# Context values of the last key block: three 32-column pieces beside self-attention in place of part of each values step in cross-attention

## The chip, the cores and the metric

The kernel runs on one core of a Trainium2 chip. The metric is the device time of one execution in microseconds (us). Beside the timed runs there is one profiled execution; its span runs from the first to the last instruction, and its own time is a little longer than the span.

The engines are named as in the profile: PE multiplies matrices (PEld are its weight loads), DVE, ACT and POOL work on vectors, and SP issues transfers (DMA). Each engine works through its own list in the order in which the program wrote it.

## The reference, cut to what matters

One transformer block on `x` (2 batches, 1024 rows, 256 columns, fp32) with a context (2 batches, 154 rows, 192 columns). 16 heads of 64 columns. Cut to its core:

```python
h = _layernorm(x, ln1_g, ln1_b)
x = _attention(h, h, sa_wq, sa_wk, sa_wv, sa_wo, sa_bo) + x
h = _layernorm(x, ln2_g, ln2_b)
x = _attention(h, cond_emb, ca_wq, ca_wk, ca_wv, ca_wo, ca_bo) + x
h = _layernorm(x, ln3_g, ln3_b)
a, gate = jnp.split(h @ ff_w1 + ff_b1, 2, axis=-1)
x = (a * gelu(gate)) @ ff_w2 + ff_b2 + x
```

In the second attention keys and values come from the context: `v = cond_emb @ ca_wv`, 154 rows of 1024 columns for each batch. The change concerns how these values are made.

## The kernel before, in words

**Stages.** Self-attention runs from about 17 to 710 us, cross-attention to about 918 us, the gated feed-forward to the end. All work is fp32, and every list is written out by hand, so that the order of the Python calls is the order on each engine.

**Self-attention.** The outer loop goes over 128 slots `p`. Eight slots make a unit, and a unit is one batch and one pair of heads (16 units, `ui`, counted from 0; units 0 to 7 are batch 0). I count the slots of a unit from 0 as `n`. Each slot computes scores of two row groups (L483, 32 matmuls in 64x32 tiles, into two PSUM tiles named `s`), then DVE takes their maximum (L645), ACT the exponents (L494), and one slot later the two halves of the keys are joined: a transfer exchanges maxima and sums (L504, SP), POOL computes `dd`, `zz` and `den` (L512 to L520), ACT `ee` (L516), DVE a reciprocal (L591), and POOL scales (L595). DVE turns the probabilities (L609) two slots after their scores.

What stands between two slots' scores on PE depends on `n`. In slots 2, 3, 6 and 7 it is the product with the values (`weigh`, L530). In slots 0, 1, 4 and 5 `run_work` puts in work of the next unit: queries, keys (both L352) and values (L383) in slots 0, 1 and 4, and in slot 5, from unit 2 on, two output pieces (`out_piece`, L457), whose results DVE adds to `x` some slots later (L464). Steps of the next normalization go beside them in slots 4 and 5. POOL adds biases (L310) in some slots. `load_ahead` issues the next weights on SP (L132) in slots 2, 3 and 7. All small accumulators live in two pools of two PSUM banks each, `mm_tile` and `sum_tile`; L530 uses both banks of `sum_tile`.

**Cross-attention.** 48 slots `c`, three per unit. A slot computes scores (L772), DVE the maximum (L777), ACT the exponents (L788), POOL scales (L799), and DVE turns (L815) into a ring `pT_ca` of three units. SP regroups a unit's turned probabilities with eight transfers (L832). The product with the values (`cross_values`, L851, results `poc`) of unit `ui` stands in the second slot of unit `ui + 2`, in 64x64 tiles, in two parts: the first takes the two banks of `sum_tile`, the second those of `mm_tile`. DVE copies the results out (L864).

The 154 keys are held as five blocks of 32 (the last one padded). Blocks 0 to 3 are weighed in regrouped pairs; the last block is weighed from the ring directly, and its values must stand on all four groups of 32 partitions.

**`context_values`** (L723 to L756) makes the values of two pairs of heads (256 columns) of one batch. It is called eight times: for unit 0 near the end of self-attention, and for units 2, 4, ... 14 in the second slot of the unit. It clears two planes of the tile `v` on DVE (L729) and runs four matmuls of 96x128 weights and 256 moving columns (L733): two for keys 0 to 127, and two for keys 32 to 159, of which only the last block is used. ACT copies the first 128 keys out (L742, two halves) and the last block from partitions 96 to 127 (L743). Then SP issues two transfers for the other halves (L745) and three that spread the last block over the other partition groups (L750). These go through the list `later`, from which each slot takes two entries.

In the second slot of an even unit, PE's order around it is: one output piece (L457, into `sum_tile`), `context_values` (L733, into `mm_tile`), a second output piece (L457, `mm_tile`), then `cross_values` (L851). DVE adds the two output pieces (L464) after clearing `v`.

**Weights.** `load_weights("ca", pr, "v")` loads 256 columns of `ca_wv` for each call. `load_keys` loads columns of `ca_wk` into a buffer with the tag `ck` for `context_keys` (L717), in self-attention's unit 0 and again in unit 14.

The lines that the change alters:

```python
        for n, k0 in enumerate((0, TP - P)):
            for c in range(2):
                nc.tensor.matmul(
                    pv[:, n * VC:(n + 1) * VC], lhsT=ctxT[:, c, b * TP + k0:b * TP + k0 + P],
                    rhs=wsl["ca", pr, "v"][:, c, :], start=(c == 0), stop=(c == 1),
                )
```

Of the kernel before, what the change touches and what calls it, by code (L numbers as in the profile page):

```python
# [8 lines left out]
F32 = mybir.dt.float32  # L9
# [4 lines left out]
P = 128  # L14
# [4 lines left out]
def tile_transformer_block(ctx: ExitStack, tc: tile.TileContext, a: dict, out: bass.AP):  # L19
    nc = tc.nc  # L20
    x, cond = a["x"], a["ctx_768"]
    w = {k[len("L0_xattn_"):]: v for k, v in a.items() if k.startswith("L0_xattn_")}

    B, S, D = x.shape
    T, DC = cond.shape[1:]
    DA = w["sa_wq"].shape[1]
    DF = w["ff_w2"].shape[0]
    DH = 64
    NPAIR = DA // (2 * DH)
# [6 lines left out]
    HR = P // 2  # L36
    NH = D // HR
    CC = DC // 2
    KP = T // 2
    KB = 32  # L40
    NB = -(-T // KB)
    VC = 2 * P
    HB = 512
    QG = 2 * KB
    TP = NB * KB
    NM = P // QG
# [5 lines left out]
    SH = GH // 2  # L52
# [4 lines left out]
    const = ctx.enter_context(tc.tile_pool(name="const", bufs=1))  # L57
    one = ctx.enter_context(tc.tile_pool(name="one", bufs=1))
    wpool = ctx.enter_context(tc.tile_pool(name="w", bufs=1))
# [8 lines left out]
    def mm_tile(name):  # L68
        return ps_m.tile([P, HB], F32, tag="mm", name=name)
# [36 lines left out]
    for n in names[:2]:  # L106
        for r0 in range(0, P, HR):
            (nc.scalar if n == names[0] else nc.sync).dma_start(
                out=cols[r0:r0 + HR, row_of[n]:row_of[n] + NH],
                in_=w[n].rearrange("(r p) -> p r", p=HR),  # L110
# [13 lines left out]
    def load_slice(name, c0, n, p):  # L124

        own = w[name][:, c0:c0 + n]
        if p != HR:
            return load_rows(wpool, name[3:], f"{name}_{c0}", own, p)
        t = wpool.tile(
            [P, NH, n], F32, tag=name[3:], name=f"{name}_{c0}", bufs=2 if name[3:] == "wq" else 1)  # L130
        for r0 in range(0, P, HR):
            nc.sync.dma_start(out=t[r0:r0 + HR], in_=own.rearrange("(c p) f -> p c f", p=HR))  # L132
        return t

    wsl, wo = {}, {}

    def load_weights(kind, pr, what):
        if kind == "sa" or what == "q":
            wsl[kind, pr, what] = load_slice(f"{kind}_w{what}", pr * P, P, HR)
        elif pr % 2 == 0:  # L140
            wsl[kind, pr, what] = load_slice(f"{kind}_w{what}", pr * P, VC, CC)

# [22 lines left out]
    for n in names[2:]:  # L165
        own = rows[row_of[n] - n_cols:row_of[n] - n_cols + n_of[n], :]
        p = HR if n in twice else P
# [13 lines left out]
    ctxT = const.tile([CC, 2, B * TP], F32, tag="ctxT", name="ctxT")  # L181
# [10 lines left out]
    def turn_context(b):  # L192
        pc = spare["bank"](f"pc{b}")
        for c in range(2):
            for i in range(2):
                nc.tensor.transpose(
                    pc[:CC, c * T + i * KP:c * T + (i + 1) * KP],
                    cn[b][:, i, c * CC:(c + 1) * CC], ident[:KP, :KP],
                )
        return lambda: nc.scalar.copy(  # L200
            ctxT[:, :, b * TP:b * TP + T], pc[:CC, :2 * T].rearrange("p (c k) -> p c k", c=2)
        )

    hT, vs, qk, oT = {}, {}, {}, {}

# [338 lines left out]
    def run(piece):  # L544
        done = piece()
        if done is not None:
            (adds if getattr(done, "adds", False) else stores).append(done)
# [165 lines left out]
    def context_keys(pr, bank):  # L713
# [6 lines left out]
            )  # L720
        return lambda: nc.scalar.copy(kT[:, pr, :], pk[:, :B * TP])

    def context_values(b, pr):  # L723

        v = vs["ca", b, pr // 2] = pt_.tile([P, NM + 2, VC], F32, tag="V", name=f"v_ca{b}_{pr}")
        nc.vector.memset(v[:, NM:, :], 0.0)  # L729
        pv = mm_tile(f"pv_ca{b}_{pr}")  # L730
        for n, k0 in enumerate((0, TP - P)):
            for c in range(2):
                nc.tensor.matmul(  # L733
                    pv[:, n * VC:(n + 1) * VC], lhsT=ctxT[:, c, b * TP + k0:b * TP + k0 + P],
                    rhs=wsl["ca", pr, "v"][:, c, :], start=(c == 0), stop=(c == 1),
                )
        last = P // KB - 1

        def store():
            for n in range(NM):  # L740
                own = slice(n * QG, (n + 1) * QG)
                nc.scalar.copy(v[own, n, :], pv[own, :VC])  # L742
            nc.scalar.copy(v[last * KB:, NM + last % 2, :], pv[last * KB:, VC:])  # L743
            later.insert(0, lambda: [
                nc.sync.dma_start(  # L745
                    out=v[(1 - n) * QG:(2 - n) * QG, n, :], in_=v[n * QG:(n + 1) * QG, n, :])
                for n in range(NM)
            ])
            later.insert(1, lambda: [
                nc.sync.dma_start(  # L750
                    out=v[a4 * KB:(a4 + 1) * KB, NM + a4 % 2, :],
                    in_=v[last * KB:, NM + last % 2, :])
                for a4 in range(last)
            ])

        return store  # L756
# [5 lines left out]
    def cross_first(c):  # L762
# [19 lines left out]
        def then():  # L782
            pr_ = pp_.tile([P, 2, TG, NB * KB], F32, tag="P", name=f"p_{c}")
            nc.gpsimd.memset(pr_[:, :, :, T:], 0.0)
# [50 lines left out]
    def cross_values(ui, a2):  # L835
# [10 lines left out]
        for m in range(NM + 1):  # L846
            for a4 in quarters:
                r0 = a4 // 2 * QG
                r = slice(r0, r0 + QG)
                for j in range(2):  # L850
# [3 lines left out]
                        rhs=pTc["pairs"][r, a2, m, j] if m < NM else  # L854
                        pTc["ring"][r, ui % 3, NB - 1, j, :],
                        start=(m == 0), stop=(m == NM),
# [121 lines left out]
    with tc.manual_schedule():  # L978
# [11 lines left out]
        own = [ps_s.tile([P, 2, HB], F32, tag="s", name=f"first_{r}") for r in range(2)]  # L990
# [45 lines left out]
        for p in range(SA):  # L1036
            if p % (2 * SH) == 0:
                self_beside(p // (2 * SH))
            if p == SA - SH:
                work.extend(held)  # L1040
                held.clear()
            then = self_first(p)
            flush(stores)
            late = then()
            if p >= LAG:
                turn_groups(p - LAG)
            if adds:
                adds.pop(0)()
            if late:
                late()  # L1050
            flush(kept)
            if later and (p < 4 or p % (2 * SH) in (2, 4, 6)):
                later.pop(0)()
            if p in ahead:
                ahead[p]()
            load_ahead(p)
            h, hg = divmod(p, SH)
            if h == 0 or hg < LAG:

                run_work(2 if p < SA - SH else 1, h % 2 or h == 0, sum_tile)  # L1060
                if p == LAG:
                    load_weights("sa", units[1][1], "v")
                ui, n = divmod(p, 2 * SH)
                if n == SH + 1 and ui in (1, NU - 1):

                    pr = 0 if ui == 1 else 3
                    run(lambda: context_keys(pr, sum_tile))
                    kept.extend(context_keys(pr + i, mm_tile) for i in range(1, 3 if ui == 1 else 2))
            else:
                run(lambda: self_values(h - 1, hg - LAG))  # L1070

        for c in range(CA):
            if c == 0:
                pTc["ring"] = pt_.tile(
                    [P, 2 * NK, QH // 2], F32, tag="pT", name="pT_ca"
                ).rearrange("p a b -> p (a b)")[:, :3 * 2 * NB * NT * KB].rearrange(
                    "p (u n j q) -> p u n j q", u=3, n=NB, j=2)
            if c == SH + 1:
# [7 lines left out]
            ui, n = divmod(c, len(CG))  # L1086
# [52 lines left out]
            elif n == 2:  # L1139
# [3 lines left out]
                elif ui == HP:  # L1143
                    wo["ca"] = const.tile([P, NPAIR, D], F32, tag="wo", name="ca_wo")
                    later[:0] = [lambda i=i: nc.sync.dma_start(
                        out=wo["ca"][:, i, :], in_=w["ca_wo"][i * P:(i + 1) * P, :])
# [6 lines left out]
        for k in range(FF):  # L1153
            c = CA + k
# [57 lines left out]
```

## Time and profile before

| what | us |
|---|---|
| three timed runs, median (lowest, highest) | 1115.72 (1113.64, 1117.36) |
| the profiled execution's own time | 1111.62 |
| its span | 1109.7 |
| PE busy, share of the span | 1093.7, 99% |
| DVE busy | 855.1, 77% |
| ACT busy | 628.2, 57% |
| POOL busy | 681.4, 61% |
| PE busy in 17 to 710 / 722 to 918 / 918 to 1110 | 685.5 / 195.5 / 188.3 |
| DVE busy in the same | 633.0 / 151.3 / 53.1 |

The granted TensorE clock is 1.00 throughout. PE's 99% is not PE at its peak: matmuls overlap, and their ends are modelled. A group in the profile reads: line, engine, operation, what it writes and reads, shapes and count, then busy us, mean ns of one, and the idle time of the engine before them with what ended it. Before the shapes stands the tile of the array that a PE instruction uses (64*32 is 64 rows by 32 columns). A timeline line reads: start in us, length in us, engine, line, operation, count, and in brackets the idle time before it and what ended that. "issue" is a pause for which the profile shows no wait.

### The profile page before, as it was taken

The numbers are of one execution on the slowest core, as the hardware profiler recorded it, in microseconds if no ns is written. First come the engines' busy times: TensorE is split into PE (matmuls) and PEld (weight loads), VectorE is DVE, ScalarE is ACT, GpSimd is POOL, SyncE is SP. The second block draws the span as 40 slices with busy tenths as digits, with TensorE's granted clock in tenths as the row PEclk, the third lists the DMA queues.
The fourth block names the chain that finished last, engine by engine and source line by source line (L and its number), as shares of the span: only waits on it lengthen the run. The fifth ranks groups of instructions, "written<-read, shape, count | busy, mean of one in ns | idle before, by whom it ended". The sixth has DMA issues, their size and how long they took to land.

```text
span 1109.7 us, 44860 instructions
## 1 busy us (share of the span) xinstructions
PE 1093.7 (99%) x18436; PEld 733.5 (66%) x18436; DVE 855.1 (77%) x1205; ACT 628.2 (57%) x2030; POOL 681.4 (61%) x1584
## 2 busy tenths in 40 slices
PE   8999999999999999999999999999999999999998
PEld 6555656546556566666566565576766777888887
DVE  5889999898999899999999999868777875322222
ACT  4766666766666666667667666655556553121111
POOL 2777877777877787777777777756656653220000
PEclk9999999999999999999999999999999999999999
DMA  3222212111111012011111111136665443000000
GB/s 83 67 59 57 56 28 52 43 41 42 25 40 42 23 42 47 13 43 42 23 42 33 32 33 28 38 87 158 167 164 126 113 107 77 10 11 10 20 10 19
DMA packets 102350, 59.66 MB, mean 54 GB/s; under 512 B 31994, under 2 KB 92930, under 8 KB 102146
## 3 DMA queue, kind: packets, MB, share of 16 engines
q1 hardware_dynamic: 100914, 56.15, 21.3%
q8 instruction: 145, 2.38, 0.9%
q10 hardware_dynamic: 1232, 0.66, 0.2%
q14 instruction: 59, 0.48, 0.1%
HBM read 27.12 MB, written 2.10 MB: 26 GB/s over the span
## 4 chain that ended last, share of the span: by engine, by line
PE 56%; ACT 11%; DVE 10%; POOL 8%; DMA 7%; issue 4%; SPq 4%; DVEq 0%; POOLq 0%; ACTq 0%
PE pa L933 10%; ACT p L494 10%; PE po L530 8%; PE s L483 8%; DVE st L645 6%; DMA st<-st 6%; PE py_ca L457 5%; PE pf L956 5%; PE pq_ca L352 4%; PE poc L851 4%; SPq L504 3%; POOL p L595 3%; PE sc L772 3%; PE py_sa L457 2%; PE pk_sa L352 2%
## 5 line engine op out<-in xcount | busy, mean ns | idle before, releaser
L494 ACT ACTIVATE p<-s,st 128x512 f32<-128x512 f32 x512 | 344.9, 686 | 194.0 <-DVE st L645 186.0
L595 POOL TENSOR_SCALAR p<-p,rd,ee 128x512 f32<-128x512 f32 x512 | 385.7, 768 | 46.7 <-DVE rd L591 45.4
L645 DVE TENSOR_REDUCE st<-s 128x2 f32<-128x1024 f32 x256 | 300.9, 1216 | 20.3 <-PE s L483 7.1
L609 DVE STREAM_TRANSPOSE pT<-p 128x1024 f32<-128x1024 f32 x256 | 302.3, 1218 | 0.3 <-POOL p L595 0.3
L483 PE MATMUL s<-k_sa,q_sa 64*32 64x512 f32 x4096 | 262.1, 592 | 7.4 <-ACT p L494 6.5
L530 PE MATMUL po<-pT,v_sa 64*32 64x256 f32 x8192 | 239.5, 376 | 0.9 <-DVE pT L609 0.9
L530 PEld LDWEIGHTS po<-pT,v_sa 64*32 64x32 f32 x8192 | 177.9, 106 | 70.5 <-issue 22.0
L483 PEld LDWEIGHTS s<-k_sa,q_sa 64*32 64x32 f32 x4096 | 78.8, 106 | 115.2 <-ACT p L494 66.4
L799 POOL TENSOR_SCALAR p<-p,rden 128x154 f32<-128x154 f32 x256 | 96.8, 398 | 76.0 <-DVE rden L796 75.6
L788 ACT ACTIVATE p<-sc,neg 128x154 f32<-128x154 f32 x256 | 96.2, 405 | 83.1 <-DVE rden L796 78.0
L942 DVE SCALAR_TENSOR_TENSOR u<-pa,cols,gate 128x256 f32<-128x256 f32 x64 | 31.0, 484 | 123.1 <-ACT gate L939 123.1
L933 PE MATMUL pa<-hT_ln,wf 128*128 128x256 f32 x512 | 121.1, 380 | 0.2 <-ACT p L788 0.2
L939 ACT ACTIVATE gate<-pa,cols 128x256 f32<-128x256 f32 x64 | 30.3, 474 | 147.8 <-PE pa L933 146.1
L933 PEld LDWEIGHTS pa<-hT_ln,wf 128*128 128x128 f32 x512 | 96.7, 190 | 14.0 <-issue 0.8
L494 ACT ACTIVATION_READ_ACCUMULATOR p<-s,st 128x1 f32 x512 | 103.8, 203 | 0.0
L383 PEld LDWEIGHTS pv_sa<-sa_wv,hT_ln 64*128 64x128 f32 x1024 | 59.0, 188 | 14.6 <-issue 5.9
L956 PE MATMUL pf<-wf,u 128*128 128x256 f32 x256 | 64.7, 379 | 0.0
L518 POOL TENSOR_TENSOR zz<-ee,st 128x8 f32<-128x8 f32 x128 | 25.9, 202 | 61.5 <-ACT ee L516 61.5
L383 PE MATMUL pv_sa<-sa_wv,hT_ln 64*128 64x128 f32 x1024 | 62.4, 276 | 0.1
L457 PE MATMUL py_sa<-sa_wo,o_sa 128*128 128x256 f32 x256 | 59.7, 385 | 0.0
L457 PE MATMUL py_ca<-ca_wo,o_ca 128*128 128x256 f32 x256 | 59.7, 381 | 0.0
L457 PEld LDWEIGHTS py_sa<-sa_wo,o_sa 128*128 128x128 f32 x256 | 47.3, 190 | 17.9 <-ACT v_sa L392 8.4
(87 smaller groups left out, 1265.4 us busy)
## 6 DMA issues: line engine op xcount, KB each, us to landing
wf<-pT_ca SPq DMA_DIRECT2D x128, 128.0 KB, 2.4
st<-st SPq DMA_DIRECT2D x512, 1.0 KB, 1.8
v_sa<-v_sa SPq DMA_DIRECT2D x32, 256.0 KB, 3.5
sa_wq<-in_L_xattn_sa_wq_dram SPq DMA_DIRECT2D x32, 128.0 KB, 3.0
sa_wk<-in_L_xattn_sa_wk_dram SPq DMA_DIRECT2D x32, 128.0 KB, 3.0
sa_wv<-in_L_xattn_sa_wv_dram SPq DMA_DIRECT2D x32, 128.0 KB, 3.1
ca_wq<-in_L_xattn_ca_wq_dram SPq DMA_DIRECT2D x32, 128.0 KB, 3.3
wf<-in_L_xattn_ff_w_dram SPq DMA_DIRECT2D x12, 256.0 KB, 4.0
```

The lines of the kernel that those rows point to most:

```text
L383: nc.tensor.matmul(pv[r][:, i * P:(i + 1) * P], lhsT=h[own, c, i * P:(i + 1) * P], rhs=wt[own, c, :], start=(c == 0), stop=(c == NH - 1), ...
L457: nc.tensor.matmul(py[:, e * D:(e + 1) * D], lhsT=o[:, i, (t + e) * P:(t + e + 1) * P], rhs=wo[kind][:, g * HP + i, :], start=(i == 0), st ...
L483: nc.tensor.matmul(sc[a4 * KB:(a4 + 1) * KB, j, :], lhsT=q[r, c:c + KB], rhs=k[r, h * HB:(h + 1) * HB], start=True, stop=True, tile_positi ...
L494: nc.scalar.activation(pr[:, j, :], sc[:, j, :], AF.Exp, bias=st[:, 0, 0, i, j:j + 1], accum_out=st[:, 0, 1, i, j:j + 1],)
L530: nc.tensor.matmul(po[a2][d:d + KB, :QH // 2], lhsT=v[r, t, e, d:d + KB], rhs=pT[r, d // DH * NK + n, :], start=(t == 0 and e == 0), stop= ...
L595: nc.gpsimd.tensor_scalar(pr[:, j, :], pr[:, j, :], rd[:, c:c + 1], ee[:, 0, c:c + 1], op0=ALU.mult, op1=ALU.mult,)
L609: nc.vector.transpose(halves[h][:, :, c:c + KB], groups.pop(0).rearrange("p j (n k) -> p (j n) k", k=KB))
L645: nc.vector.tensor_reduce(st[:, 0, 0, i, :], sc[i], AX.X, ALU.max, negate=True)
L788: nc.scalar.activation(pr_[:, j, i, :T], sc[:, j, i * T:(i + 1) * T], AF.Exp, bias=neg[:, j, i:i + 1], accum_out=den[:, j, i:i + 1],)
L799: nc.gpsimd.tensor_scalar(pr_[:, j, i, :T], pr_[:, j, i, :T], rden[:, j, i:i + 1], 1.0, op0=ALU.mult, op1=ALU.mult,)
L933: nc.tensor.matmul(pa[:, half, :TF * P], lhsT=w1[:, c, half * DF + f * P:half * DF + (f + 1) * P], rhs=h[:, c, t0 * P:(t0 + TF) * P], star ...
L956: nc.tensor.matmul(sums[blk][i][:, :D], lhsT=sums[blk, "u"][:, f, i * P:(i + 1) * P], rhs=w2[:, f, :], start=(f == 0), stop=(f == NF - 1),)
```

## The change

A new step, `context_ends`, computes the last key block's values for both batches and all heads, in three pieces, within self-attention's units 5, 6 and 7. A piece covers 192, 192 and 128 columns in each half of the 1024 columns. The stationary operand is the last 32 keys of a batch (96x32); the four combinations of batch and half go to the four groups of 32 partitions of one `sum_tile` bank, so that one piece is eight matmuls. ACT then copies the bank into `ends`, a tile that stays on chip (128 partitions, 512 columns). A piece's columns of `ca_wv` are loaded by two transfers in slot 0 of the unit, into the buffer `ck`; the matmuls stand in slot 5, after that slot's `run_work`, and the copy is made in the next slot ahead of its exponents.

`context_values` keeps the matmuls for keys 0 to 127 alone. Its copy of the last block is gone, and the three transfers of L750 become four, which read `ends`.

```diff
+    EC = 3 * HR
...
+    ends = const.tile([P, DA // 2], F32, tag="ends", name="ends")
...
+    def load_ends(f, n):
+
+        t = wpool.tile([CC, 2, 2, n], F32, tag="ck", name=f"ca_wv_{f}")
+        own = w["ca_wv"].rearrange("(c p) (h f) -> p c h f", p=CC, h=2)
+        for c in range(2):
+            nc.sync.dma_start(out=t[:, c], in_=own[:, c, :, f:f + n])
+        wsl["ends", f] = t
+
+    def context_ends(f, n, bank):
+
+        pe = bank(f"pe_{f}")
+        for c in range(2):
+            for b in range(B):
+                for half in range(2):
+                    r0 = (2 * b + half) * KB
+                    nc.tensor.matmul(
+                        pe[r0:r0 + KB, :n], lhsT=ctxT[:, c, (b + 1) * TP - KB:(b + 1) * TP],
+                        rhs=wsl["ends", f][:, c, half, :], start=(c == 0), stop=(c == 1),
+                        tile_position=(0, r0),
+                    )
+        return lambda: nc.scalar.copy(ends[:, f:f + n], pe[:, :n])
...
-        for n, k0 in enumerate((0, TP - P)):
-            for c in range(2):
-                nc.tensor.matmul(
-                    pv[:, n * VC:(n + 1) * VC], lhsT=ctxT[:, c, b * TP + k0:b * TP + k0 + P],
-                    rhs=wsl["ca", pr, "v"][:, c, :], start=(c == 0), stop=(c == 1),
-                )
-        last = P // KB - 1
+        for c in range(2):
+            nc.tensor.matmul(
+                pv[:, :VC], lhsT=ctxT[:, c, b * TP:b * TP + P],
+                rhs=wsl["ca", pr, "v"][:, c, :], start=(c == 0), stop=(c == 1),
+            )
+        half, c0 = divmod(pr * P, DA // 2)
+        last = (2 * b + half) * KB
...
-            nc.scalar.copy(v[last * KB:, NM + last % 2, :], pv[last * KB:, VC:])
...
-                    in_=v[last * KB:, NM + last % 2, :])
-                for a4 in range(last)
+                    in_=ends[last:last + KB, c0:c0 + VC])
+                for a4 in range(P // KB)
...
                 ui, n = divmod(p, 2 * SH)
+                f = (ui - NPAIR // 2 - 1) * EC
+                if n == 0 and 0 <= f < DA // 2:
+                    load_ends(f, min(EC, DA // 2 - f))
+                elif n == SH + 1 and 0 <= f < DA // 2:
+                    run(lambda: context_ends(f, min(EC, DA // 2 - f), sum_tile))
```

## The prediction

> **What bounds the kernel now.** I read the page's chain of waits first, then the busy table by stage, the chain written out in order of time, and the timeline where the change puts or takes work.
>
> ```profile
> PE 56%; ACT 11%; DVE 10%; POOL 8%; DMA 7%; issue 4%; SPq 4%; DVEq 0%; POOLq 0%; ACTq 0%
> ```
>
> PE is over half of the chain, but not all of it. By stage it looks different. From 722 us to the end of cross-attention (918 us) the chain, in order of time, is PE nearly throughout. Around the second call of `context_values` it reads (start, us, what):
>
> ```profile
> 739.98 1.92 PE py_sa L457 x8
> 741.90 1.73 PE pv_ca L733 x8
> 743.63 1.73 PE py_sa L457 x8
> 745.36 2.75 PE poc L851 x48
> ```
>
> One piece of PE work follows the other, and what is taken out there lets the rest move up. The feed-forward stage after it stays on PE (its ACT waits 146 us for PE), so a gain in cross-attention reaches the end. In self-attention two loops run almost level: PE, whose slots repeat to a hundredth (4.98, 5.17, 5.53 us in many units), and scores, DVE maximum, ACT exponents, POOL scaling. Which of them is late must be read slot by slot.
>
> **What is removed.** Eight calls of `context_values` each lose two matmuls, an ACT copy and a wait on it.
>
> ```profile
> L733 PE MATMUL pv_ca<-ca_wv,ctxT 96*128 96x256 f32 x64 | 15.2, 380 | 0.0
> L743 ACT COPY v_ca<-pv_ca 32x256 f32<-32x256 f32 x8 | 2.9, 364 | 0.9 <-DVE v_ca L729 0.7
> ```
>
> 64 rows for 32 matmuls: each fp32 matmul is two rows. The eight rows of one call take 1.73 us in the chain, so 0.216 us a row, and four rows gone are 0.86 us. One call lies in self-attention's last slots (691 us); after it PE waits 0.84 us for ACT exponents, so I count nothing there. Of the seven in cross-attention, PE's next step (`poc`, L851) also needs the bank that DVE's first addition (L464) empties. In the call at 822 us that addition ends long before:
>
> ```profile
> 821.57 1.70 PEld L733 LDWEIGHTS pv_ca<-ca_wv,ctxT 96*128 96x128 f32 x8
> 822.53 0.63 DVE L464 TENSOR_TENSOR x<-py_ca,x 128x512 f32<-128x512 f32 x1
> 823.30 1.70 PEld L457 LDWEIGHTS py_ca<-ca_wo,o_ca 128*128 128x128 f32 x8
> 825.33 0.64 PEld L851 LDWEIGHTS poc<-wf,v_ca 64*64 64x64 f32 x16 [0.33 <-issue]
> ```
>
> It ends at 823.16, 2.17 us ahead of `poc`; in four others it ends 1.1 to 2.2 us ahead. These five give 0.86 each, **4.3 us**. In the calls at 769 and 875 us DVE is full with normalization copies:
>
> ```profile
> 771.57 0.62 DVE L464 TENSOR_TENSOR x<-py_ca,x 128x512 f32<-128x512 f32 x1
> ...
> 772.48 0.64 PEld L851 LDWEIGHTS poc<-wf,v_ca 64*64 64x64 f32 x16 [0.33 <-DVE x L464]
> ```
>
> The addition ends at 772.19, 0.29 us before `poc`, and at 875 us 0.17 before. There DVE becomes the wait; I take 0.2 and 0.1 us. Bounds for the pair: 0 (DVE binds now) and 1.7 (DVE moves up with PE). The ACT copy (0.36 us) is behind PE everywhere: nothing.
>
> SP gets one DMA more per call: the three of L750 take 1.84 us of issue at 825.35, so 0.6 us more, ahead of the eight transfers of L832 that regroup the probabilities. These are issued until 2 us or more before their `poc`, except for unit 13: its last leaves SP at 913.04, its second half of `poc` starts at 915.54, and one landing takes a median 2.4 us from its issue. With SP 0.2 us later (its start is 0.4 earlier, since ACT's copy comes earlier) and PE up to 0.86 us earlier, I take a wait of 0.2 us (0 to 0.86). Cross-attention in sum: 4.3 + 0.3 - 0.2 = **4.4 us gained**.
>
> **What is added.** In slot 5 of units 5, 6 and 7, after two output pieces (L457) and ahead of the next scores: eight matmuls, 16 rows, weights of 32 columns, moving 192, 192 and 128 columns, four of them on different columns of the array. No row of before has 96x32 weights. The nearest is `poc`: weights 64x64, four tiles at once. Its 48 rows of 256 columns run in 12 groups of four, 0.216 us a group, and the next scores' weights come 2.75 us after the first: 12 x 0.216 + 0.16 for draining at the change of tiles. Scaled to 192 columns a group takes 0.162 us: 4 x 0.162 + 0.16 = **0.81 us**; to 128 columns 4 x 0.108 + 0.16 = **0.59**. The other end is no overlap at all, 16 groups: 2.75 and 1.89 us. I take the low end, since every tiled row of this trace (L352, L530, L851) overlaps as many rows as it has tiles. Nothing below zero is possible; the work is new in this slot.
>
> What this does to the end: the next slot's DVE maximum (L645) can start 1.25 us after the first score weights. In unit 6 it does:
>
> ```profile
> 308.34 3.32 PEld L457 LDWEIGHTS py_sa<-sa_wo,o_sa 128*128 128x128 f32 x16 [0.84 <-issue]
> 311.99 0.18 PEld L483 LDWEIGHTS s<-k_sa,q_sa 64*32 64x32 f32 x16 [0.33 <-ACT ee L516]
> 313.24 2.36 DVE L645 TENSOR_REDUCE st<-s 128x2 f32<-128x1024 f32 x2 [0.61 <-DMA v_sa<-v_sa]
> ```
>
> DVE idles 0.61 us before it although the reciprocal is done; PE is late, and DVE has no idle time in the rest of that slot and the next. All 0.81 us reach the path. In unit 5 the same distance is 2.12 us (268.27 to 270.39), 0.87 to spare: PE's 0.81 is hidden, and if that cover went, it would cost 0.81. In unit 7:
>
> ```profile
> 354.26 0.18 PEld L483 LDWEIGHTS s<-k_sa,q_sa 64*32 64x32 f32 x16 [0.33 <-issue]
> ...
> 355.80 2.36 DVE L645 TENSOR_REDUCE st<-s 128x2 f32<-128x1024 f32 x2
> ```
>
> 1.54 us, 0.29 to spare: 0.59 - 0.29 = 0.30. **Self-attention loses 0 + 0.81 + 0.30 = 1.1 us**; without overlap 1.88 + 2.75 + 1.60 = 6.2.
>
> The other additions are covered. ACT copies 128x192 once per piece, about 0.37 us by L630's 128x256; it waits for PE with the next exponents behind it, but ACT idles 2.64 us before those in unit 6. L530's second bank now waits for that copy, which ends about 0.6 us before L530 starts. SP issues two loads in slot 0, some 1.3 us by the two of L132, after that slot's exchange (L504); the next exchange is a slot later, and the loads are used five slots later. If they held SP up, POOL's `dd` would wait.
>
> A rule of the Trainium skill speaks against the change. At 825.33 and 828.08 PE's weights pause 0.33 and 0.39 us where the tile shape changes. "TensorEngine Tiling (Array Packing)", section Tiling Modes, says that changing the tiling mode drains the engine, and each piece brings a third shape between two; my terms hold 0.16 us of it as `poc` shows it, and with a full second pause of 0.33 self-attention would lose about 1.6 us. "TensorE: Matmul & The Clock Gate", section Measured speedup vs the span model, gives 2.38 for three column tiles instead of 3; by that ratio four would give some 3.2, the pieces about 0.97 us as an estimate, and the loss about 1.5. No run here shows either.
>
> **Sum.** 1.1 - 4.4 = **-3.3 us**, made against the profiled execution: span 1109.7, its own time 1111.62 with 1.9 us around it, giving 1108.3. That execution lies below all three timed runs (1113.64 to 1117.36); against their median of 1115.72 the same step gives **1112.4**.
>
> **Rivals.**
> - *PE's whole gain arrives*: seven calls at 0.86 = 6.0, DVE moving up with PE in both tight calls, 0.5 lost in self-attention: -5.5 us, 1110.2. For it: DVE's full stretch before 769 us was itself set off by PE. Against: DVE has no idle time from 764 to 772 us.
> - *Another engine becomes the bound in cross-attention*: ACT is busy without a gap from 844 to 851 us and SP's regroup comes later; half of the five calls' gain is lost: -1.1 us, 1114.6. Against it: PE's waits for others add up to a few us in 196.
> - *The four column tiles do not overlap*: all share the 96 rows, which no row here does. 6.2 us lost against 4.4: +1.8, 1117.5, **slower**. It decides from a group of some 1.85 us on (1.85 - 0.87 + 1.85 + 1.85 - 0.29 = 4.4). Against: three tile shapes here overlap in full.
> - *The change doesn't do what it says* is excluded by the instruction order: each engine's list differs only by the rows counted above.
>
> **How the numbers follow.** Forecast (-2 to -4.6 us) 0.55; whole gain 0.15; another bound 0.20; no overlap 0.10. 0.3% of the median is 3.35 us, about what a measurement of this kernel can tell from no change, and the forecast lies on that edge: somewhat under half of it counts as faster (0.26), with most of the whole gain (0.14): faster 0.40; slower by over 0.3% needs groups of some 3 us or a bad draw: 0.04; within: 0.56. Range: -6.0 to +1.8 from the cases, with the timed runs' scatter of about 2 us partly inside: 1109.0 to 1117.0.
>
> **What would show it.** L733 falls to half its rows; the new rows in slot 5 run in groups of four at 0.16 us; the maximum after them moves by 0 / 0.8 / 0.3 us; from 722 us to the end the stretch is 4.4 us shorter, with DVE's addition as the wait ahead of `poc` at two calls. Wrong would be: 16 rows one after another; the slots after unit 5 longer; or a cross-attention stretch that shrinks by under 3 us, with a new wait for ACT or L832 ahead of PE.

## The result and the profile after

Twenty runs of each kernel gave a median of 1114.76 us before (1112.18 to 1117.36) and **1113.38 us after** (1110.51 to 1116.66). The ratio is 0.9987 with a 95% interval of 0.9978 to 0.9997: 1.4 us less, between 0.3 and 2.5. The forecast was 3.3 us less. The sign was right, the gain a little under half.

The lines of `kernel.py` after the change stand further down: L462 is the output piece (L457 before), L469 its addition (L464), L488 the scores (L483), L535 the product with the values (L530), L650 the maximum (L645), L509 the exchange (L504), L877 `poc` (L851), L858 the regroup (L832). L759 is `context_values`, L743 the matmuls of a piece, L748 its copy, L776 the transfers from `ends`. A slot's scores are 16 matmuls, which the profile counts as 32 rows. Runs further down whose file differs by a line or two have their own numbers: L879 is `poc` and L860 the regroup there.

The chain of waits, by engine, of the profile after:

```profile
PE 63%; ACT 9%; DMA 7%; POOL 7%; DVE 7%; issue 3%; SPq 3%; DVEq 0%; POOLq 0%; ACTq 0%
```

PE's share rose from 56%. That is not by itself a sign of success or failure. The changed groups (out<-in, shape, count | busy us, mean ns | idle before them):

```profile
L759 PE MATMUL pv_ca<-ca_wv,ctxT 96*128 96x256 f32 x32 | 8.3, 382 | 0.0
L743 PE MATMUL pe<-ca_wv,ctxT 96*32 96x192 f32 (+1 forms) x48 | 2.4, 314 | 0.0
L748 ACT COPY ends<-pe 128x192 f32<-128x192 f32 (+1 forms) x3 | 0.9, 294 | 1.5 <-PE pe L743 1.5
```

Half the rows of `context_values` are gone, as the change says. The chain in order of time around its second call (start, us, what):

```profile
746.94 1.92 PE py_sa L462 x8
748.86 0.86 PE pv_ca L759 x4
749.73 1.73 PE py_sa L462 x8
751.46 2.75 PE poc L877 x48
```

1.73 us became 0.86 and the rest moved up. In unit 6 of self-attention, the timeline of PE's weight loads around the piece (start, length, what, idle time before):

```profile
314.21 0.48 PEld L743 LDWEIGHTS pe<-ca_wv,ctxT 96*32 96x32 f32 x16 [0.33 <-issue]
315.00 0.18 PEld L488 LDWEIGHTS s<-k_sa,q_sa 64*32 64x32 f32 x16 [0.30 <-issue]
```

The piece takes 315.00 - 314.21 = 0.79 us, where 0.81 was forecast, and DVE, next to need the scores, waits for it:

```profile
316.25 1.23 DVE L650 TENSOR_REDUCE st<-s 128x2 f32<-128x1024 f32 x1 [1.39 <-DMA st<-st]
```

Its idle time was 0.61 us before. The line names a transfer as what ended the wait, but the scores did: the maximum starts 1.25 us after their first weights here, in before, and in nine of the twelve other profiles (1.28 to 1.33 in the rest), whatever the idle time. So the parts did what they were to do, and yet the two profiled executions read the wrong way round: spans of 1109.7 before and 1112.5 after. A table by stretch says why. Each stretch runs from the first weight load of a score matmul to that of another, read from the timelines; the third column is a second profile of the changed kernel.

| stretch, us | before | after | after, again |
|---|---|---|---|
| start to unit 0 | 17.60 | 17.60 | 17.46 |
| self-attention, units 0 to 3 | 171.72 | 173.30 | 174.33 |
| unit 4 | 45.09 | 44.94 | 45.14 |
| **units 5 to 7** | 130.00 | 132.16 | 131.96 |
| unit 8, slots 0 to 3 | 22.03 | 20.83 | 20.74 |
| from there to the end of unit 14 | 281.42 | 284.24 | 281.46 |
| **unit 15, first seven slots** | 36.50 | 37.83 | 37.47 |
| from there to cross-attention's unit 2 | 30.28 | 30.70 | 31.05 |
| **cross-attention, units 2 to 14** | 173.91 | 169.32 | 169.21 |
| **unit 15, its first two slots** | 8.40 | 9.18 | 8.98 |
| unit 15's third slot and the feed-forward | 192.75 | 192.40 | 192.38 |

Over all 14 profiles of this study units 0 to 3 take 171.7 to 177.1 us and units 8 to 14 302.2 to 308.5. A comparison of two single profiles is lost in that. The stretches that the change touches repeat much better, and they are what the experiments read. Cross-attention gains 4.6 to 4.7 us, as much as the forecast's terms without SP's wait (4.3 + 0.3), and gives 0.6 to 0.8 back in unit 15, where the forecast had 0.2. Units 5 to 7 lose about 2, of which 1.2 to 1.3 come back at once, in the first four slots of unit 8. Unit 15 of self-attention, in which nothing is changed ahead of its slot 5, is about 1.2 longer. Of unit 15 of cross-attention I read the second slot, which holds unit 13's `poc`; the expectations below call it the unit's last slot, since it is the last that ends at another score.

### The profile page after: what moved, and what is told of

Same layout as the page of the kernel before. It is cut to its first block, busy times and chain, and to the rows that moved or that the text cites. A ratio compares the mean times of both kernels' runs of the same rounds, so it can differ in the third digit from the quotient of the medians.

```text
span 1112.5 us, 44903 instructions
## 1 busy us (share of the span) xinstructions
PE 1092.5 (98%) x18452; PEld 732.9 (66%) x18452; DVE 855.3 (77%) x1205; ACT 626.1 (56%) x2025; POOL 684.7 (62%) x1584
## 4 chain that ended last, share of the span: by engine, by line
PE 63%; ACT 9%; DMA 7%; POOL 7%; DVE 7%; issue 3%; SPq 3%; DVEq 0%; POOLq 0%; ACTq 0%
PE pa L959 10%; PE po L535 10%; PE s L488 10%; ACT p L499 8%; DMA st<-st 6%; PE pf L982 5%; PE py_ca L462 5%; DVE st L650 4%; PE pq_ca L357 4%; PE poc L877 4%; SPq L509 3%; PE py_sa L462 3%; PE sc L798 3%; PE pv_sa L388 3%; PE pk_sa L357 3%
## 5 line engine op out<-in xcount | busy, mean ns | idle before, releaser
L650 DVE TENSOR_REDUCE st<-s 128x2 f32<-128x1024 f32 x256 | 300.9, 1216 | 22.6 <-PE s L488 9.7
L488 PE MATMUL s<-k_sa,q_sa 64*32 64x512 f32 x4096 | 263.9, 593 | 8.6 <-ACT p L499 7.6
L535 PE MATMUL po<-pT,v_sa 64*32 64x256 f32 x8192 | 241.2, 376 | 1.7 <-DVE pT L614 1.4
L535 PEld LDWEIGHTS po<-pT,v_sa 64*32 64x32 f32 x8192 | 178.1, 106 | 71.9 <-issue 19.2
L488 PEld LDWEIGHTS s<-k_sa,q_sa 64*32 64x32 f32 x4096 | 82.6, 106 | 113.5 <-ACT p L499 61.9
L462 PE MATMUL py_sa<-sa_wo,o_sa 128*128 128x256 f32 x256 | 59.7, 385 | 0.0
L462 PE MATMUL py_ca<-ca_wo,o_ca 128*128 128x256 f32 x256 | 59.7, 381 | 0.0
L357 PE MATMUL pk_sa<-hT_ln,sa_wk 64*32 64x512 f32 x960 | 58.2, 591 | 1.0 <-DMA st<-st 0.8
```

The costliest lines, as they stand in the source:

```text
L357: nc.tensor.matmul(pq[r][f:f + m, at:at + n], lhsT=wt[own, c, f:f + m], rhs=h[own, c, t0:t0 + n], start=(c == 0), stop=(c == NH - 1), tile ...
L462: nc.tensor.matmul(py[:, e * D:(e + 1) * D], lhsT=o[:, i, (t + e) * P:(t + e + 1) * P], rhs=wo[kind][:, g * HP + i, :], start=(i == 0), st ...
L488: nc.tensor.matmul(sc[a4 * KB:(a4 + 1) * KB, j, :], lhsT=q[r, c:c + KB], rhs=k[r, h * HB:(h + 1) * HB], start=True, stop=True, tile_positi ...
L535: nc.tensor.matmul(po[a2][d:d + KB, :QH // 2], lhsT=v[r, t, e, d:d + KB], rhs=pT[r, d // DH * NK + n, :], start=(t == 0 and e == 0), stop= ...
L650: nc.vector.tensor_reduce(st[:, 0, 0, i, :], sc[i], AX.X, ALU.max, negate=True)
```

## The experiments

Ratios are against before, run on the same chip in the same series, with 95% intervals; microseconds are the ratio times before's median there (1118.46, 1112.58 and 1114.88 us in the three series). Theory A: two orders, not PE's time, took the missing gain. Theory B: PE's time for the pieces is simply lost, and the waits shown beside it are no causes.

**One part alone.** The first run keeps `context_values` as before and adds the pieces; the second keeps the new `context_values` and has no pieces, so that the last key block's values are left out. Both edits are against the changed kernel; the first is cut.

```diff
         pv = mm_tile(f"pv_ca{b}_{pr}")
-        for c in range(2):
-            nc.tensor.matmul(
-                pv[:, :VC], lhsT=ctxT[:, c, b * TP:b * TP + P],
...
+        for n, k0 in enumerate((0, TP - P)):
+            for c in range(2):
+                nc.tensor.matmul(
+                    pv[:, n * VC:(n + 1) * VC], lhsT=ctxT[:, c, b * TP + k0:b * TP + k0 + P],
...
```

```diff
+                if ui == 6 and n == SH + 1:
+                    nc.vector.memset(ends, 0.0)
-                if n == 0 and 0 <= f < DA // 2:
-                    load_ends(f, min(EC, DA // 2 - f))
-                elif n == SH + 1 and 0 <= f < DA // 2:
-                    run(lambda: context_ends(f, min(EC, DA // 2 - f), sum_tile))
```

> The three pieces are made and copied, but context_values is that of before, so that ends is written and not used. The forecast's own step: +1.1 us against before (0 + 0.81 + 0.30). Theory A, from the slots of after: unit 5's piece is hidden in its own slot, but ACT's copy of it stands behind two normalization copies (L265), and L535 waits for its bank, so about 0.7 us come back one slot later; with 0.8 in unit 6 and 0.3 to 0.6 in unit 7 the sum is +1.8 to +2.2 us. Theory B: every piece costs its whole PE time whatever stands beside it, 0.79 + 0.79 + 0.57 = +2.15 us. The timed runs cannot tell A from B here; in the trace A has slot 6 of unit 5 at 5.6 us, B at 4.98.

> No pieces and no loads of theirs: ends is set to zero once on DVE in unit 6, so the last key block's values are left out; context_values is that of after. The forecast's step: -4.4 us against before. Theories A and B, from after's slots: the second slot of the seven even units is 4.6 us shorter in sum, and unit 15's last slot gives 0.8 back, so -3.8 us. If the pieces cost more than their slots show, this run would lie at the same -3.8 while pieces_alone lies above +2.2.

Measured: pieces alone 1.0025 (1.0012 to 1.0038), **+2.8 us** (1.3 to 4.2). The cut alone 0.9952 (0.9936 to 0.9969), **-5.4 us** (-7.2 to -3.5). With pieces alone, units 2 to 14 of cross-attention took 173.95 us, as before to 0.04; with the cut alone 169.30, and unit 15's second slot 3.83 in place of 4.52, so the 0.8 that both theories had given back was not. The two parts add up to -2.6; the whole has -1.4 in the first measurement and -2.3 in another. The forecast's +1.1 for the pieces is below the interval: the miss is mostly there.

**ACT's copy.** In unit 5 the piece was forecast to be hidden. At its own slot it is: DVE's first maximum there starts 1.39 us after the scores' first weights (2.12 before), and from one slot's maximum to the next it is 6.46 us, before 6.40. Then, one slot on, PE's weight loads of the changed kernel read:

```profile
269.73 0.48 PEld L743 LDWEIGHTS pe<-ca_wv,ctxT 96*32 96x32 f32 x16 [0.33 <-issue]
270.52 0.18 PEld L488 LDWEIGHTS s<-k_sa,q_sa 64*32 64x32 f32 x16 [0.30 <-issue]
...
273.21 2.96 PEld L535 LDWEIGHTS po<-pT,v_sa 64*32 64x32 f32 x116 [0.80 <-ACT ends L748]
```

L535 stops for its second bank until ACT has copied the piece out. ACT, in the same profile:

```profile
271.87 1.09 ACT L265 ACTIVATE xn_ln<-x,off_ln,rstd_ln 128x256 f32<-128x256 f32 x2 [0.86 <-DVE off_ln L251]
272.86 0.30 ACT L748 COPY ends<-pe 128x192 f32<-128x192 f32 x1
273.17 0.69 ACT L499 ACTIVATE p<-s,st 128x512 f32<-128x512 f32 x1
```

The scores behind the piece start at 270.52, so its matmuls were through by about then, and ACT stood idle for 0.86 us. But the copy is written behind two normalization copies (L265), and these wait for DVE. Only unit 5 has them there. The experiment writes the copy ahead of them and changes nothing else:

```diff
-                run_work(2 if p < SA - SH else 1, h % 2 or h == 0, sum_tile)
+                if n == SH + 1 and 0 <= f < DA // 2:
+                    run_work(2, 0)
+                    context_ends(f, min(EC, DA // 2 - f), sum_tile)()
+                    run_work(0, 1, sum_tile)
+                else:
+                    run_work(2 if p < SA - SH else 1, h % 2 or h == 0, sum_tile)
```

> After, with ACT's copy of a piece written ahead of that slot's normalization steps instead of at the head of the next slot; PE's order is unchanged. Theory A: L535 no longer waits for ACT in slot 6 of unit 5, the slot goes from 5.60 back to 4.98 us, DVE's 0.70 us of idle time before the second maximum of that unit's slot 7 goes, and the time is 0.6 to 0.7 us below after. Theory B: slot 6 may get shorter, but what the piece took on PE is lost anyway, and the time from slot 5 of unit 5 to slot 5 of unit 6 stays at 44.5 us, 0.8 more than before.

Measured: 0.9990 (0.9977 to 1.0002), which cannot tell 0.6 us. The slot can. ACT's lines, then PE's, of this run:

```profile
275.57 0.30 ACT L748 COPY ends<-pe 128x192 f32<-128x192 f32 x1
276.52 1.09 ACT L265 ACTIVATE xn_ln<-x,off_ln,rstd_ln 128x256 f32<-128x256 f32 x2 [0.65 <-DVE off_ln L251]
```

```profile
276.42 0.15 PEld L535 LDWEIGHTS po<-pT,v_sa 64*32 64x32 f32 x8 [0.28 <-issue]
276.85 3.18 PEld L535 LDWEIGHTS po<-pT,v_sa 64*32 64x32 f32 x120 [0.28 <-issue]
```

The wait is gone and slot 6 takes 4.98 us (5.60, 5.57, 5.70, 5.71 and 5.71 in the five profiles with the late copy). Units 5 to 7 take 131.40 to 131.58 us in the three profiles with the early copy and loads by SP, and a mean of 132.20 in the five with the late one: 0.7 us. It is not given back by slot 4 of unit 8: from unit 5's start to there the late copy takes 152.71 to 153.62 us, the early one 152.26 to 152.42. Theory A holds here. The three kernels without pieces take 152.03 to 152.78 over the same stretch, so with the early copy nothing of the pieces' PE time is left four slots behind them. Theory B's 44.5 us from slot 5 of unit 5 to slot 5 of unit 6 became 43.9.

**The transfers from `ends`.** In the changed kernel the second half of unit 13's `poc` stops in its middle:

```profile
917.70 0.36 PEld L877 LDWEIGHTS poc<-wf,v_ca 64*64 64x64 f32 x4
918.63 0.44 PEld L877 LDWEIGHTS poc<-wf,v_ca 64*64 64x64 f32 x10 [0.57 <-DVE pT_ca L841]
```

The profile names DVE's L841, which ran from 917.82 us on. But L841 turns unit 14's probabilities there, which this product does not read, and PE's own wait instruction in the trace (917.95 to 918.60) is for the last two transfers of the regroup. What was late is the regroup on SP, behind four transfers (L776) in place of three. And its first transfer took 1.42 us to issue, where most take 0.6:

```profile
910.59 1.42 SPq L858 DMA_DIRECT2D wf<-pT_ca  x1
```

The experiment lets the four transfers of the last call of `context_values` go out after that regroup:

```diff
+            if (b, pr) == units[NU - 2]:
+                later.insert(1, lambda: None)
-            later.insert(1, lambda: [
+            later.insert(1 + ((b, pr) == units[NU - 2]), lambda: [
```

> After, with the last call's four transfers from ends issued behind the eight that regroup unit 13, in place of ahead of them. Theory A: the regroup starts 2.5 us earlier on SP, the wait inside the second half of poc of unit 13 goes, and unit 15's last slot is 3.7 us as in before (4.52 in after); the time is 0.8 us below after. Theory B: the wait is there because PE came up by 0.86 us and the regroup did not, whose turned probabilities are ready no sooner; the slot stays above 4.2 us and the time within 0.3 us of after.

Measured: 0.9991 (0.9972 to 1.0011), again too coarse, in an execution with much scatter elsewhere. Unit 15's second slot is 3.74 us, exactly that of before, and PE's line has no pause. The regroup starts 7.8 us ahead of unit 13's `poc` (6.0 in the changed kernel), 1.8 us earlier where 2.5 was expected:

```profile
925.99 0.80 PEld L879 LDWEIGHTS poc<-wf,v_ca 64*64 64x64 f32 x16
```

Theory A holds for the order of the transfers. They cost 0.78, 0.58, 0.78 and 0.33 us in the four profiles that have pieces and this order (slots of 4.52, 4.32, 4.52 and 4.07 us). Why it is so much, the cut alone tells: it has the fourth transfer too, but no long issue at the head of the regroup (0.64 us), and its slot is 3.83. The fourth transfer, with PE 0.86 us earlier, costs 0.1 us. The rest goes with the long issue: 1.35 to 1.53 us at the regroup's first transfer in the three profiles with 0.58 and 0.78, 1.13 at its second in the one with 0.33. With the late transfers there is a long one too (1.61, its fourth), but it ends in time.

**Do the tiles overlap because of the list's order?**

```diff
-        for c in range(2):
-            for b in range(B):
-                for half in range(2):
+        for b in range(B):
+            for half in range(2):
+                for c in range(2):
```

> After, with the order of a piece's eight matmuls changed so that both chunks of one tile follow each other: four rows on one group of 32 columns, then four on the next. The forecast's case without overlap has 16 rows at 0.162 us, 2.6 us for a piece. If rows overlap only with neighbours in the list, a piece takes about (4 x 3 + 1) x 0.162 + 0.14 = 2.25 us, slot 5 of unit 5 is 7.8 us instead of 6.32; if PE looked past the row that waits, it would stay at 6.32.

One execution of 1112.26 us; the slots are 6.34, 6.33 and 6.12, after's 6.32, 6.32 and 6.10:

```profile
268.56 0.50 PEld L743 LDWEIGHTS pe<-ca_wv,ctxT 96*32 96x32 f32 x16 [0.33 <-issue]
269.37 0.18 PEld L488 LDWEIGHTS s<-k_sa,q_sa 64*32 64x32 f32 x16 [0.30 <-issue]
```

0.81 us in place of 0.79. Slot 6 of unit 6 behind the piece is 4.98 us in both, so PE does not pay later either. The order of the list does not matter here, and my price of 2.25 us for it was wrong.

**The changed kernel again, and with three orders mended.** `mended` joins the early copy and the late transfers, and lets DVE clear `v` behind its two additions:

```diff
-        nc.vector.memset(v[:, NM:, :], 0.0)
...
         def store():
+            nc.vector.memset(v[:, NM:, :], 0.0)
```

> The changed kernel once more, on the same chip as the next three, to see which slots repeat and to have a ratio beside theirs. By the slots of the first profile: pieces -2.0 to -2.2 us, cross-attention +3.8 us, so 1.6 to 1.8 us below before; slot 5 of units 5, 6, 7 at 6.32, 6.32, 6.10 us, slot 6 of unit 5 near 5.6, unit 15's last slot 4.52. If slot 6 of unit 5 or unit 15's last slot come out as before (4.98, 3.74), these two were scatter of one execution and not part of the change.

> After with three orders changed: ACT's copy of a piece ahead of the normalization steps, the last call's transfers from ends behind the regroup of unit 13, and the clearing of v's two planes on DVE behind the additions (L469) in place of ahead of them. Theory A: 0.6 us from the first, 0.8 from the second; the third is worth 0.4 us in each of units 4 and 12, because DVE's addition is what poc waits for there (the slot goes from 9.60 to 9.2 and from 10.31 to 9.9). Sum 2.2 us below after. Theory B (PE's work alone sets these slots, and the idle times shown beside them are not causes): each slot stays, and the time is within 0.3 us of after.

> mended once more, on the same chip as the next three. By the slots of its first profile it is 2.0 us below after, so 4 us or a little more below before (first ratio 0.9960). Slot 6 of unit 5 at 4.98, the second slots of units 4 and 12 of cross-attention at 9.09 and 9.75, unit 15's last at 3.74; unit 15 of self-attention at 37.5 to 37.8 us, as in every kernel so far that loads the pieces on SP (36.50 in before, 36.14 without pieces).

Measured: after again 0.9979 (0.9967 to 0.9990), -2.3 us; the slots repeat (6.32, 6.31, 6.10; 5.57), but for unit 15's (4.32 in place of 4.52). Mended **0.9960** (0.9948 to 0.9972), -4.5 us, and in the later series 0.9969 (0.9955 to 0.9982), -3.5. On one chip the medians are 1112.58 before, 1110.40 after, 1109.02 mended. It has the lowest ratio of the versions that leave nothing out, though its interval overlaps that of `moved` below, and it is ahead of both kernels. What the third edit shows, in the changed kernel and then in `mended`, at unit 4's `poc`:

```profile
777.74 0.19 PEld L877 LDWEIGHTS poc<-wf,v_ca 64*64 64x64 f32 x4 [0.33 <-issue]
778.38 0.41 PEld L877 LDWEIGHTS poc<-wf,v_ca 64*64 64x64 f32 x10 [0.45 <-DVE x L469]
```

```profile
774.40 0.76 PEld L879 LDWEIGHTS poc<-wf,v_ca 64*64 64x64 f32 x16 [0.33 <-issue]
```

The wait for DVE's addition is the one that the forecast put there. With the clearing out of the way the slots fall from 9.60 to 9.09 us and from 10.31 to 9.75, 0.5 us each (0.4 expected): DVE was the bound in just these two calls.

**Other slots for the pieces.** In `moved` they stand where PE waits for exponents: unit 4's slots 0 and 5, unit 5's slot 0.

```diff
+                piece = {(4, 0): 0, (4, SH + 1): 1, (5, 0): 2}.get((ui, n))
...
+            f = {(3, 6): 0, (4, 2): EC, (4, 6): 2 * EC}.get(divmod(p, 2 * SH))
+            if f is not None:
+                load_ends(f, min(EC, DA // 2 - f))
```

> mended, with the three pieces in other slots: slot 0 and slot 5 of unit 4 and slot 0 of unit 5, with their loads one to two slots ahead. In before and after PE waits 0.5 to 1.2 us for exponents in nearly every slot of unit 4 and in the first two of unit 5; in units 6 and 7 it hardly waits. Theory A: the pieces take up those waits, the time from unit 4's start to unit 6's start stays at that of before (89.3 us; 90.4 in after, where it holds one piece), and the time is 1.2 to 1.6 us below mended, so 5 us below before. Theory B: a piece costs its PE time wherever it stands; nothing gained over mended. A piece between two 64x32 shapes may also take longer than 0.79 us, since there are two changes of shape around it in place of one.

Measured: 0.9973 (0.9963 to 0.9984), -3.0 us, not the -5 of theory A. The slots are on A's side: units 4 to 7 take 175.58 us (before 175.09, `mended` 176.43; the two other kernels without pieces 175.91 and 175.98), although a piece between two 64x32 shapes has a longer pause before it than behind an output piece (0.33):

```profile
195.29 0.48 PEld L743 LDWEIGHTS pe<-ca_wv,ctxT 96*32 96x32 f32 x16 [0.84 <-ACT p L499]
```

The line names ACT's exponents; but the same 0.84 us stands before output pieces and values behind 64x32 rows, with other names or none. The profiled spans are level (1107.4 and 1107.5). So the move saves 0.8 us in its own units, and the timed runs do not show it. By slot 4 of unit 8 0.4 to 0.6 us of it is left (196.87 us from unit 4's start; 197.45 and 197.23 in `mended`'s two profiles). No profile here shows where the rest goes.

**What the loads do to unit 15.** The last series asks what the pieces cost once their orders are mended, and whether their six loads on SP lengthen unit 15.

```diff
-            nc.sync.dma_start(out=t[:, c], in_=own[:, c, :, f:f + n])
+            nc.scalar.dma_start(out=t[:, c], in_=own[:, c, :, f:f + n])
```

> mended without pieces and without their loads (ends is set to zero once; the last key block's values are left out): the floor that the other three can reach. Theory A: the pieces cost mended 1.1 us in units 5 to 7, and their six loads another 1.2 us in unit 15, since they shift which transfers of SP get a long issue (1 to 1.6 us in place of 0.6): without them unit 15 is 36.1 to 36.5 us, and the time is 2.3 us below mended. Theory B (unit 15's 1.2 us belong to cross-attention's new order or are scatter): 1.1 us below mended, unit 15 at 37.5.

> mended, with the pieces' six loads issued by ACT in place of SP, in the same slots. SP's list in self-attention is then that of before. Theory A: the exchange (L509) of slot 6 of unit 14 is issued in 2.4 us in place of 2.8 to 3.4, unit 15 is back at 36.1 to 36.5 us, and the time is 1.2 us below mended. Theory B: unit 15 stays at 37.5 and the time within 0.3 us of mended, or above it, because ACT spends 1.2 us per piece on issuing ahead of its copies of the queries.

> moved, with the six loads issued by ACT. Theory A: pieces in unit 4 and at the start of unit 5 cost nothing (units 4 to 7 took 175.58 us in moved, 175.09 in before, 176.43 in mended), and unit 15 is back at 36.1 to 36.5: as fast as no_pieces within its scatter, 1 us below loads_act. Theory B, from moved's timed runs, which lay 1.1 us above mended's while its profile did not: something outside units 4 to 7 pays for the move, and it lies above loads_act by about 1 us again.

Measured: no pieces 0.9942 (0.9927 to 0.9958), **-6.5 us**; loads by ACT 1.0001 (0.9986 to 1.0015); moved with loads by ACT 0.9978 (0.9959 to 0.9997), -2.5. Between `mended` and no pieces lie 3.0 us by the ratios of this series (each known to about 1.5 us either way); by the slots 0.5 in units 5 to 7 (131.43 against 130.91) and 2.0 in unit 15 (37.93 against 35.95). Over all profiles, unit 15's seven slots:

| kernels | us |
|---|---|
| without pieces (three: before, cut alone, no pieces) | 35.95 to 36.50 |
| with pieces (eleven) | 37.45 to 37.93, one 41.50 |

In the same profiles the exchange for unit 14's slot 6, which goes out early in slot 7 and whose four transfers are issued by SP, differs. After, no pieces, and loads by ACT:

```profile
668.20 3.02 SPq L509 DMA_DIRECT2D st<-st  x4
```

```profile
667.03 2.41 SPq L509 DMA_DIRECT2D st<-st  x4
```

```profile
673.24 3.17 SPq L509 DMA_DIRECT2D st<-st  x4
```

Every kernel with pieces has one long issue (0.9 to 1.6 us) in this exchange, and every one without has it in the exchange before (0.86 to 1.03). With it the next exchange starts 6.1 to 6.6 us after its own slot's first score weights, without it 5.6. But moving the loads to ACT did not bring it back, so theory A fell as I had put it: it is not the six places on SP's list. The long issue goes with the pieces and their loads together, whichever engine issues the loads; no run has the one without the other.

What goes with its place, the DMA view shows. It lists the packets by queue, and one queue is named instruction (queue, kind: packets, MB, share of 16 engines): first the whole changed kernel, then its exchange above (668.2 to 671.3 us), then that of loads by ACT (673.2 to 676.5):

```profile
q8 instruction: 146, 2.39, 0.9%
```

```profile
q8 instruction: 1, 0.02, 2.2%
```

```profile
q8 instruction: 1, 0.02, 2.3%
```

For the exchange of no pieces (667.0 to 669.5) the view lists no such packet. Over the 14 profiles, 877 of the 899 issues on SP of 1.0 us or more overlap a packet of this queue, and 1357 of the 11711 under 0.7 us. The 145 or 146 packets come with 37262 to 37422 instructions on PE's list, one for every 256. I read them as PE's list being loaded, which is an inference from that count. Their places then depend on the place in PE's list, and a kernel with pieces has 96 instructions more ahead of unit 8 (48 weight loads, 48 rows), on whichever queue the loads stand. In slot 7 of unit 14 the packet starts 1.3 to 2.0 us into the slot in all eleven profiles with pieces, inside the exchange, and 3.4 to 3.9 us into it in the three without, behind it.

Unit 15 is not alone in this. In every profile with pieces units 9 and 13 are longer than in any without (43.03 to 44.52 us against 42.52 to 42.98, and 43.46 to 45.13 against 43.05) and unit 12 is shorter (42.74 to 44.00 against 44.17 to 44.70). From slot 4 of unit 8 to slot 7 of unit 15 the kernels with pieces take 318.9 to 322.9 us (one 329.3), those without 317.0 to 319.5: about 3 us by the medians, which is what the timed runs put on the pieces. That the shifted packets and long issues bring this is likely; it is not proved, since no run moved them with the pieces in place. As theory B's second half said, ACT paid for the issues: slot 1 of units 5, 6 and 7 rose from 5.15 to 5.23 us to 5.7 to 6.0, and units 5 to 7 to 134.21.

## Why the forecast was half right

- **The removed rows: right.** 0.86 us at five calls was 0.86 or 0.87; 0.2 and 0.1 at the two calls where DVE becomes the wait were 0.23 and 0.06 (14.23 to 14.00 and 14.79 to 14.73 us). DVE's part is shown by `mended`.
- **The price of a piece: right.** 0.81 and 0.59 us were 0.79 and 0.57. Four rows on four column tiles overlap in full. The rule in "TensorEngine Tiling (Array Packing)", section Tiling Modes, that a change of mode drains the engine agrees with the trace, which shows two pauses, 0.33 and 0.30 us, in place of one of 0.33. The estimate of 0.97 us from "TensorE: Matmul & The Clock Gate", section Measured speedup vs the span model, is not met: 0.79 decides.
- **Unit 5 "hidden": the step that failed.** The 0.87 us to spare was real, and DVE's maximum did not move. What failed is the sentence that L530's second bank waits for a copy that ends about 0.6 us before it is needed. I had placed the copy by ACT's idle time, in unit 6, and not by what is written ahead of it on ACT in unit 5. It ended 0.6 us too late instead, and the early copy gave 0.7 us back. With it, the forecast's "hidden" holds.
- **Units 6 and 7, 0.81 and 0.30: right only for a few slots.** The slots grew by 0.79 and by the whole 0.57. The 0.29 to spare in unit 7 stands in all three profiles without pieces (0.29 to 0.38), but in none of the nine with a piece there, where DVE waits 0.36 to 1.03 us for PE. That all of unit 6's 0.81 reaches the path did not hold: by slot 4 of unit 8 the kernels with the early copy are level with those without pieces, so the 1.1 us that I had put on the pieces there came to nothing.
- **SP's 0.2 at unit 13: mis-sized.** It was 0.33 to 0.78 us, within my bound (0 to 0.86). The fourth transfer that I had counted is worth 0.1; what I had not counted is that one issue in some fourteen takes 1.0 to 2.1 us, and that one of these could fall on this regroup.
- **Not foreseen at all:** about 3 us from slot 4 of unit 8 to unit 15 of self-attention, 1.2 of them in unit 15. I costed this at nothing, because SP's two loads hold up no exchange in their own slots. In the profiles it shows up to eight units later.

Counted with the slots, the change gains 4.6, loses 0.6 at unit 13 and 1.7 by the end of unit 7 (132.20 against a mean of 130.50 in the three profiles without pieces there). Of these 1.7, 1.2 are back by slot 4 of unit 8, and from there to unit 15 some 3 are lost. That would leave next to nothing, where the timed runs say 1.4 and 2.3. Sums over single profiles do not close better than this, because the units from 8 on scatter by 2 us and more.

So that the total came out inside the range has luck in it: the pieces cost less than forecast where I had priced them, and more where I had put nothing. The first measurement (-1.4) lies outside the forecast's own band (-2 to -4.6) and nearest to the figure of "another engine becomes the bound" (-1.1), though that is not what happened; the second (-2.3) lies inside the band. Of the rivals, "no overlap" is excluded, "the whole gain" failed at the two calls where DVE binds, and "another engine becomes the bound" has a true part in SP's regroup alone; five of the seven calls gave their full 0.86 us, so ACT held up none of these.

## What to carry to other kernels

Work that fits into an engine's spare time still has to leave its buffer: follow the instruction that empties it through its own engine's list, slot by slot, and ask what stands ahead of it there and what that waits for. When a total scatters by more than the effect, compare the stretches and slots that repeat, and mend one order at a time; here that turned -1.4 to -2.3 us into -3.5 to -4.5. Added work is not free because its engine and its queue have room. Nor is a loss at the end of the changed stretch final: here 1.2 us of it were back four slots later, and about 3 us were lost further on, in units that the pieces do not touch. Run the kernel without the new work as well, and compare far behind it.

## What the runs showed of the hardware

A piece's time did not change when its sixteen rows were listed tile by tile (0.81 against 0.79 us). The pause of PE's weight loads before a change of tile shape depends on what came before: 0.33 us from 128x128 to 96x32, 0.30 from 96x32 to 64x32 behind rows of 192 columns (0.20 behind 128), 0.84 from 64x32 with 512 columns to 96x32 (0.84 to 128x128 as well). On SP the median transfer takes 0.59 us to issue, and about one in fourteen 1.0 to 2.1 us. Nearly all of these long ones (877 of 899) overlap a packet of the queue named instruction, which moves one packet of 16 KB for every 256 instructions of PE. Adding 96 instructions to PE's list moved those packets, and with them the long issues, hundreds of microseconds later.
